# A pairwise outer-product batch norm: stores in halves, ScalarE adding the shift for eight pairs, short rows multiplied on VectorE

## The chip, the cores and the metric

One core of a Trainium2 chip runs the whole program. The metric is device time in microseconds (us). The kernel before takes 1895.81 us (median of three runs, 1895.78 to 1895.99). Engines are named as the profile names them: PE (TensorE), DVE (VectorE), ACT (ScalarE), POOL (GpSimd) and SP (SyncE, which only issues transfers here).

## The reference

There are 1024 samples with 39 fields of 16 numbers in each of two inputs, xi and xj. For each of the 741 pairs (row r, column c < r) the outer product of xj[r] and xi[c] is formed, normalised over the batch, and multiplied elementwise by a 16x16 matrix W:

```python
cross = xj[:, rows, :, None] * xi[:, cols, None, :]
mean = jnp.mean(cross, axis=(0, 2, 3), keepdims=True)
var = jnp.mean(jnp.square(cross - mean), axis=(0, 2, 3), keepdims=True)
normed = (cross - mean) * jax.lax.rsqrt(var + BN_EPS)
normed = normed * gamma[None, :, None, None] + beta[None, :, None, None]
out = normed[:, :, None, :, :] * W[None, None, :, :, :]
```

The output is 1024 x 741 x 256 numbers of four bytes, 777 MB; the inputs are about 6 MB. With a scale s and a shift t for each pair, the result is ((xj * (s * xi)) + t) * W.

## The kernel before, in words

The 1024 samples lie on 128 partitions, eight (called t) in each. A tile is one row r for two of the eight t, so each row has four tiles, and a tile holds 2r pairs of 256 numbers in each partition. Row 19 comes first, and then the rows go in couples: for r = 20, 21, ... 38 and each t0 the big tile (r, t0) is followed by the small tile (38 - r, t0). Row 38 has no small tile. Rows 34 to 37 are thus coupled with rows 4 to 1, and those rows are the last but one stage of the kernel; row 38 is the last.

The result is built in place in `y_sb`, which has two halves. One couple (76 pairs in all) fills a half and the next couple takes the other half, so a half is written again only when the stores of the couple before the last have landed.

The first 60 us compute s and t (statistics, not touched here). Then each tile goes through four steps:

- `scale_xi(n)` (L153): POOL multiplies xi by s into a tile `xs`. The pool that holds `xs` has two buffers (L74), taken in turn, so the `xs` of tile n + 2 lies where that of tile n lay.
- `products(n)` (L165): for each t and each of 16 values of i, `xs` is multiplied by one number of xj per partition. ACT does 12 (11 in rows over 31) of the 16 i (L137), POOL the other 4 (5) (L139).
- `finish(n)` (L214): for most pairs DVE does (y + t) * W in one instruction per pair (L233). For the last 13% of the pairs POOL adds t (one instruction each, L221) and then multiplies by W (one instruction for all of them, L225).
- `store(n, c0, c1)` (L173): SP issues the transfers. Rows to 24 leave in one piece, rows 25 to 31 in two, rows over 31 in three; in rows over 24 the last piece goes as one transfer for each t, the others as one for both.

The order of all instructions is the order in which the program emits them (`tc.manual_schedule()`), and each engine works through its own list. The loop (L433) does, for tile n: `scale_xi(n + 2)`, `finish(n)`, `products(n + 1)`. Seen from POOL, for a big tile B and its small tile S this reads: scale the next big tile's xi; add and weigh its share of B; products of S; scale the next small tile's xi; add and weigh its share of S, if there is one; products of the next B. An `xs` that is written again makes POOL wait until the products of two tiles before have been read out of it.

Of the kernel before, what the change touches and what calls it, by code (L numbers as in the profile page):

```python
# [8 lines left out]
AF = mybir.ActivationFunctionType  # L9
ALU = mybir.AluOpType  # L10
# [4 lines left out]
T = 2  # L15


ONE, TWO = 24, 31
FIRST_PIECES = ((0, 2, 8, 19), (0, 9, 19))


POOL_I, POOL_I_LONG = 4, 5
POOL_SHARE = 0.13

LOADS = (0, 1, 2, 4, 8)


ROW_GROUPS = (
# [5 lines left out]
def tile_pair_outer_batchnorm(  # L34
# [15 lines left out]
    nc = tc.nc  # L50
    P = nc.NUM_PARTITIONS
    NB, F, E = xi.shape
    NT = NB // P
    EE = E * E
# [7 lines left out]
    tiles = [(mid, t0, t0 // T * half // 2) for t0 in range(0, NT, T)]  # L62
# [14 lines left out]
    xj_sb = cpool.tile([P, NT, F, E], F32, name="xj_sb")  # L77
    w_sb = cpool.tile([P, 1, EE], F32, name="w_sb")
    st_sb = cpool.tile([P, 2, NP], F32, name="st_sb")
    s_sb = st_sb[:, 0:1].unsqueeze(3)  # L80
    t_sb = st_sb[:, 1]
# [39 lines left out]
    banks = [psp.tile([P, 512], F32, name=f"ps{n}") for n in range(7)]  # L121
    ps_s, ps_c, ps_g = banks[0], banks[1], banks[2:5]

    ps_st = banks[5:7] + ps_g
    stt = nc.vector.scalar_tensor_tensor

    def view(n):
        r, _, u = tiles[n]
        return y_sb[:, u : u + T * r, :].rearrange("p (t n) e -> p t n e", t=T)

    def product(n, engine, t, i, src):

        r, t0, _ = tiles[n]
        y = view(n).rearrange("p t n (i j) -> p t n i j", j=E)[:, t, :, i, :]
        scale = xj_sb[:, t0 + t, r, i : i + 1]
        if engine is nc.scalar:
            nc.scalar.activation(y, src, AF.Copy, scale=scale)  # L137
        else:
            engine.tensor_scalar(y, src, scale, 1.0, ALU.mult, ALU.mult)  # L139
# [13 lines left out]
    def scale_xi(n):  # L153
        r, t0, _ = tiles[n]
        n0 = first[r]
        xs = scaled.tile([P, T, r, E], F32, tag="xs", name=f"xs_{r}_{t0}")
        nc.gpsimd.tensor_tensor(  # L157
            xs,
            xi_sb[:, t0 : t0 + T, 0:r, :],
            s_sb[:, :, n0 : n0 + r, :].to_broadcast([P, T, r, E]),  # L160
            ALU.mult,
        )
        xs_of[n] = xs

    def products(n):  # L165

        xs = xs_of.pop(n)
        split = E - (POOL_I_LONG if tiles[n][0] > TWO else POOL_I)
        for t in range(T):
            for i in range(E):  # L170
                product(n, nc.scalar if i < split else nc.gpsimd, t, i, xs[:, t])

    def store(n, c0, c1):  # L173
        r, t0, _ = tiles[n]
        n0 = first[r]

        step = 1 if r > ONE and c1 == r else T
        for t in range(0, T, step):
            nc.sync.dma_start(  # L179
                out_v[:, t0 + t : t0 + t + step, (n0 + c0) * EE : (n0 + c1) * EE],  # L180
                view(n)[:, t : t + step, c0:c1, :].rearrange("p t n e -> p t (n e)"),
            )

    def affine(n):

        r = tiles[n][0]
        y = view(n)
        for c in range(r):
            s_c = st_sb[:, 0, first[r] + c : first[r] + c + 1]
            t_c = t_sb[:, first[r] + c : first[r] + c + 1]  # L190
            if c % 2 == 0:
                nc.scalar.activation(y[:, :, c, :], y[:, :, c, :], AF.Identity, bias=t_c, scale=s_c)  # L192
            else:
                nc.gpsimd.tensor_scalar(  # L194
                    y[:, :, c, :], y[:, :, c, :], s_c, t_c, ALU.mult, ALU.add
                )

    def weigh(n, bounds):

        y = view(n)  # L200
        for c0, c1 in zip(bounds, bounds[1:]):
            nc.vector.tensor_tensor(  # L202
                y[:, :, c0:c1, :],
                y[:, :, c0:c1, :],
                w_dve.unsqueeze(1).to_broadcast([P, T, c1 - c0, EE]),
                ALU.mult,
            )
            store(n, c0, c1)

    def bounds(r):  # L210
        pieces = 1 + (r > ONE) + (r > TWO)
        return tuple(q * r // pieces for q in range(pieces + 1))

    def finish(n):  # L214

        r = tiles[n][0]
        n0 = first[r]
        y = view(n)
        split = r - int(r * POOL_SHARE + 0.5)
        for c in range(split, r):  # L220
            nc.gpsimd.tensor_scalar(  # L221
                y[:, :, c, :], y[:, :, c, :], t_sb[:, n0 + c : n0 + c + 1], 1.0, ALU.add, ALU.mult
            )
        if split < r:
            nc.gpsimd.tensor_tensor(  # L225
                y[:, :, split:r, :],
                y[:, :, split:r, :],
                w_sb.unsqueeze(1).to_broadcast([P, T, r - split, EE]),
                ALU.mult,
            )  # L230
        for c0, c1 in zip(bounds(r), bounds(r)[1:]):
            for c in range(c0, min(c1, split)):
                stt(  # L233
                    y[:, :, c, :],
                    y[:, :, c, :],
                    t_sb[:, n0 + c : n0 + c + 1],
                    w_dve.to_broadcast([P, T, EE]),
                    ALU.add,
                    ALU.mult,
                )  # L240
            store(n, c0, c1)

    with tc.manual_schedule():
        for t0, t1 in zip(LOADS, LOADS[1:]):
            nc.sync.dma_start(xj_sb[:, t0:t1], xj_v[:, t0:t1])
# [157 lines left out]
        for r0, r1, bank, _ in ROW_GROUPS:  # L403
            n0, n1 = first[r0], first[r1 - 1] + r1 - 1
# [13 lines left out]
        def apply(group):  # L418
            ps, n0, n1 = spread_of[group]
            nc.vector.tensor_mul(ps[:, 1], ps[:, 1], st_sb[:, 0, n0:n1])  # L420
            nc.vector.tensor_mul(st_sb[:, 0, n0:n1], ps[:, 0], st_sb[:, 0, n0:n1])
            nc.vector.tensor_add(st_sb[:, 1, n0:n1], ps[:, 1], st_sb[:, 1, n0:n1])

        apply(0)
        affine(0)
        weigh(0, FIRST_PIECES[0])
        scale_xi(2)
        apply(1)
# [4 lines left out]
        for n in range(1, len(tiles)):  # L433
            if n == 1:
                products(2)
                scale_xi(3)
                continue
            if n + 2 < len(tiles):
                scale_xi(n + 2)
            finish(n)  # L440
            for group, (_, _, _, tile_of) in enumerate(ROW_GROUPS):
                if n == tile_of:
                    apply(group)
            if n + 1 < len(tiles):
                products(n + 1)
# [28 lines left out]
```

## Time and profile before

| | |
|---|---|
| median of three runs | 1895.81 us |
| profiled execution, its own time | 1895.88 us |
| its span, first to last instruction | 1894.1 us |
| DVE busy | 1730.9 us (91%) |
| ACT busy | 1621.5 us (86%) |
| POOL busy | 1574.5 us (83%) |
| PE busy | 24.5 us (1%) |
| written to memory | 776.99 MB |
| share of the 16 DMA engines' time with packets on the output queue | 97.9% |

Busy shares are means over the whole span; the limit of a stage is read from the stage. In the timeline of the profile each line is a run of like instructions of one engine: its start and length in us, the engine, the line of the kernel, what is written and read, how many, and in brackets how long the engine had been idle and what ended that. "x10" after a shape is the number of instructions. A big tile's start on DVE is the first L233 line after an idle stretch, and the distance from one to the next is the period of a couple.

### The profile page before, as it was taken

To read this page: it belongs to the slowest core of one execution; us is meant where nothing else is said; L and a number is where in the kernel's file an instruction comes from. 1 tells how busy PE (TensorE), PEld (TensorE's weight loads), DVE (VectorE), ACT (ScalarE), POOL (GpSimd) and SP (SyncE) were. 2 spreads that over 40 slices of the span, in tenths; PEclk is the share of its full clock that TensorE was granted. 3 is DMA by queue.
4 is the path that set the end of the run, shared out by engine and by line. 5 is a ranking of instruction groups with operands and counts; after the bars stand their busy time and mean duration, and the time that the engine had idled before them with its cause. 6 is when DMAs were issued, how large, how long until landed. Compare 5 with 4: busy or idle time off the path is not lost. (4 is left out here: it accounts for less than half of the span.)

```text
span 1894.1 us, 10252 instructions
## 1 busy us (share of the span) xinstructions
PE 24.5 (1%) x128; PEld 23.1 (1%) x128; DVE 1730.9 (91%) x2609; ACT 1621.5 (86%) x3625; POOL 1574.5 (83%) x1985
## 2 busy tenths in 40 slices
PE   3100000000000000000000000000000000000000
PEld 3100000000000000000000000000000000000000
DVE  7999999998989898989898989899999999999996
ACT  8998989898989897989898989888888888888762
POOL 9797878787878787878787878898888888888972
DMA  3899999999999999999999999999999999999999
GB/s 147 362 426 430 425 430 426 427 428 422 430 424 425 424 425 425 424 426 424 423 426 424 425 424 422 424 421 421 421 421 421 418 414 420 414 418 417 417 418 389
DMA packets 67567, 783.67 MB, mean 414 GB/s; under 512 B 4896, under 2 KB 6048, under 8 KB 13728
## 3 DMA queue, kind: packets, MB, share of 16 engines
q1 hardware_dynamic: 66912, 780.46, 97.9%
q10 hardware_dynamic: 576, 2.56, 0.3%
q14 instruction: 78, 0.64, 0.1%
q8 instruction: 1, 0.02, 0.0%
HBM read 6.00 MB, written 776.99 MB: 413 GB/s over the span
## 5 line engine op out<-in xcount | busy, mean ns | idle before, releaser
L233 DVE SCALAR_TENSOR_TENSOR y_sb<-y_sb,st_sb,w_dve 128x512 f32<-128x512 f32 x2542 | 1678.7, 742 | 134.9 <-issue 133.0
L137 ACT ACTIVATE y_sb<-xs,xj_sb 128x256 f32<-128x256 f32 (+32 forms) x3544 | 1576.5, 537 | 228.4 <-DMA out_dram<-y_sb 170.3
L139 POOL TENSOR_SCALAR y_sb<-xs,xj_sb 128x560 f32<-128x560 f32 (+35 forms) x1256 | 643.0, 534 | 39.4 <-DMA out_dram<-y_sb 31.1
L225 POOL TENSOR_TENSOR y_sb<-y_sb,w_sb 128x1024 f32<-128x1024 f32 (+4 forms) x138 | 441.9, 3202 | 11.5
L157 POOL TENSOR_TENSOR xs<-xi_sb,st_sb 128x576 f32<-128x576 f32 (+37 forms) x150 | 187.8, 1252 | 225.9 <-ACT y_sb L137 213.8
L221 POOL TENSOR_SCALAR y_sb<-y_sb,st_sb 128x512 f32<-128x512 f32 x384 | 259.4, 691 | 13.1 <-ACT y_sb L137 13.1
L202 DVE TENSOR_TENSOR y_sb<-y_sb,w_dve 128x1024 f32<-128x1024 f32 (+4 forms) x5 | 20.9, 4205 | 3.9 <-ACT y_sb L192 3.9
L137 ACT ACTIVATE y_sb<-xi_sb,xj_sb 128x304 f32<-128x304 f32 x40 | 18.7, 534 | 0.1
L409 PE MATMUL ps<-y_sb 39*128 39x38 f32 (+37 forms) x76 | 16.5, 397 | 5.5 <-DVE y_sb L397 5.5
L409 PEld LDWEIGHTS ps<-y_sb 39*128 39x128 f32 x76 | 16.3, 329 | 5.7 <-issue 5.7
L192 ACT ACTIVATE y_sb<-y_sb,st_sb 128x512 f32<-128x512 f32 x20 | 14.2, 798 | 0.0
L194 POOL TENSOR_SCALAR y_sb<-y_sb,st_sb 128x512 f32<-128x512 f32 x18 | 13.5, 766 | 0.3 <-issue 0.3
L139 POOL TENSOR_SCALAR y_sb<-xi_sb,xj_sb 128x304 f32<-128x304 f32 x24 | 11.9, 528 | 0.0
L294 DVE TENSOR_REDUCE y_sb<-y_sb 128x78 f32<-128x1248 f32 x8 | 11.1, 1443 | 0.0
L288 ACT ACTIVATE y_sb<-y_sb 128x1248 f32<-128x1248 f32 x8 | 9.9, 1244 | 1.3 <-POOL y_sb L278 1.3
L272 DVE TENSOR_REDUCE y_sb<-xj_sb 128x78 f32<-128x1248 f32 (+1 forms) x5 | 5.9, 1189 | 5.5 <-DMA xj_sb<-in_r_xj_dram 5.5
L278 POOL TENSOR_TENSOR y_sb<-xj_sb,y_sb 128x1248 f32<-128x1248 f32 x4 | 9.3, 2322 | 1.9 <-ACT y_sb L322 1.9
L278 POOL TENSOR_TENSOR y_sb<-xi_sb,y_sb 128x1248 f32<-128x1248 f32 x4 | 9.3, 2329 | 0.0
L311 PE MATMUL ps<-y_sb 128*39 128x79 f32 x48 | 7.2, 339 | 16.6 <-DVE y_sb L294 16.6
L311 PEld LDWEIGHTS ps<-y_sb 128*39 128x39 f32 x48 | 6.1, 183 | 17.5 <-DVE y_sb L294 9.6
L272 DVE TENSOR_REDUCE y_sb<-xi_sb 128x78 f32<-128x1248 f32 (+1 forms) x5 | 5.9, 1186 | 0.1
L254 POOL TENSOR_SCALAR_AFFINE_SELECT y_sb<-y_sb 39x4992 f32<-39x4992 f32 x1 | 4.6, 4624 | 0.0
(45 smaller groups left out, 16.9 us busy)
## 6 DMA issues: line engine op xcount, KB each, us to landing
out_dram<-y_sb SPq DMA_DIRECT2D x32, 3072.0 KB, 13.7
out_dram<-y_sb SPq DMA_DIRECT2D x29, 2816.0 KB, 15.5
out_dram<-y_sb SPq DMA_DIRECT2D x32, 1664.0 KB, 14.3
out_dram<-y_sb SPq DMA_DIRECT2D x16, 3328.0 KB, 17.1
out_dram<-y_sb SPq DMA_DIRECT2D x12, 3840.0 KB, 17.6
out_dram<-y_sb SPq DMA_DIRECT2D x29, 1536.0 KB, 15.4
out_dram<-y_sb SPq DMA_DIRECT2D x12, 3584.0 KB, 18.4
out_dram<-y_sb SPq DMA_DIRECT2D x20, 1792.0 KB, 17.7
```

What stands on the lines that cost most here:

```text
L137: nc.scalar.activation(y, src, AF.Copy, scale=scale)
L139: engine.tensor_scalar(y, src, scale, 1.0, ALU.mult, ALU.mult)
L157: nc.gpsimd.tensor_tensor(xs, xi_sb[:, t0 : t0 + T, 0:r, :], s_sb[:, :, n0 : n0 + r, :].to_broadcast([P, T, r, E]), ALU.mult,)
L192: nc.scalar.activation(y[:, :, c, :], y[:, :, c, :], AF.Identity, bias=t_c, scale=s_c)
L194: nc.gpsimd.tensor_scalar(y[:, :, c, :], y[:, :, c, :], s_c, t_c, ALU.mult, ALU.add)
L202: nc.vector.tensor_tensor(y[:, :, c0:c1, :], y[:, :, c0:c1, :], w_dve.unsqueeze(1).to_broadcast([P, T, c1 - c0, EE]), ALU.mult,)
L221: nc.gpsimd.tensor_scalar(y[:, :, c, :], y[:, :, c, :], t_sb[:, n0 + c : n0 + c + 1], 1.0, ALU.add, ALU.mult)
L225: nc.gpsimd.tensor_tensor(y[:, :, split:r, :], y[:, :, split:r, :], w_sb.unsqueeze(1).to_broadcast([P, T, r - split, EE]), ALU.mult,)
L233: stt(y[:, :, c, :], y[:, :, c, :], t_sb[:, n0 + c : n0 + c + 1], w_dve.to_broadcast([P, T, EE]), ALU.add, ALU.mult,)
L278: nc.gpsimd.tensor_tensor(devs[n % 7], sources[x][:, t0 : t0 + T], shift[:, x : x + 1, :].unsqueeze(3).to_broadcast([P, T, F, E]), ALU.sub ...
L311: nc.tensor.matmul(acc[0:F, 0 : 2 * F + 1], lhs, fb[:, t], start=t == 0, stop=t == NT - 1)
L409: nc.tensor.matmul(ps[:, :, first[r] - n0 : first[r] - n0 + r], pick[:, r, :], stq[:, :, 0:r], start=True, stop=True,)
```

## The change

Four things change.

- `bounds`: rows over 24 leave in two pieces; there is no third piece any more for rows over 31.
- `products`: the limit from which POOL takes five of the 16 i instead of four moves from rows over 31 to rows over 33. Rows of up to 4 are no longer multiplied by ACT and POOL: DVE forms all of a t's products in one instruction, two per tile, from `xs` and from a copy of four rows of xj that ACT makes once, in PSUM (`xj_short`).
- `finish`: in rows over 33 the pairs that don't go through DVE are eight instead of four or five, and they are the last eight of the first half of the row instead of the last of the row. ACT adds t to them (eight instructions), and POOL multiplies by W in two instructions of four pairs each. Rows to 33 keep the old way.
- DVE's part in rows over 33 falls from r - 4 (row 34) or r - 5 pairs to r - 8.

```diff
-ONE, TWO = 24, 31
+ONE, LONG = 24, 33
...
-POOL_SHARE = 0.13
+POOL_SHARE, POOL_PAIRS_LONG = 0.13, 8
...
+SHORT = 4
...
+    xj_short = ps_c.rearrange("p (t r i) -> p t r i", t=NT, i=E)
...
         xs = xs_of.pop(n)
-        split = E - (POOL_I_LONG if tiles[n][0] > TWO else POOL_I)
+        r, t0, _ = tiles[n]
+        if r <= SHORT:
+            for t in range(T):
+                nc.vector.tensor_tensor(
+                    view(n)[:, t].rearrange("p n (i j) -> p n i j", j=E),
+                    xs[:, t].unsqueeze(2).to_broadcast([P, r, E, E]),
+                    xj_short[:, t0 + t, r - 1 : r, :].unsqueeze(3).to_broadcast([P, r, E, E]),
+                    ALU.mult,
+                )
+            return
+        split = E - (POOL_I_LONG if tiles[n][0] > LONG else POOL_I)
...
-        pieces = 1 + (r > ONE) + (r > TWO)
+        pieces = 1 + (r > ONE)
...
-        split = r - int(r * POOL_SHARE + 0.5)
-        for c in range(split, r):
-            nc.gpsimd.tensor_scalar(
-                y[:, :, c, :], y[:, :, c, :], t_sb[:, n0 + c : n0 + c + 1], 1.0, ALU.add, ALU.mult
-            )
-        if split < r:
+        long = r > LONG
+        p1 = r // 2 if long else r
+        p0 = p1 - (POOL_PAIRS_LONG if long else int(r * POOL_SHARE + 0.5))
+        step = POOL_PAIRS_LONG // 2 if long else r
+        for c0 in range(p0, p1, step):
+            c1 = min(c0 + step, p1)
+            for c in range(c0, c1):
+                t_c = t_sb[:, n0 + c : n0 + c + 1]
+                if long:
+                    nc.scalar.activation(y[:, :, c, :], y[:, :, c, :], AF.Identity, bias=t_c)
+                else:
+                    nc.gpsimd.tensor_scalar(
+                        y[:, :, c, :], y[:, :, c, :], t_c, 1.0, ALU.add, ALU.mult
+                    )
             nc.gpsimd.tensor_tensor(
-                y[:, :, split:r, :],
-                y[:, :, split:r, :],
-                w_sb.unsqueeze(1).to_broadcast([P, T, r - split, EE]),
+                y[:, :, c0:c1, :],
+                y[:, :, c0:c1, :],
+                w_sb.unsqueeze(1).to_broadcast([P, T, c1 - c0, EE]),
                 ALU.mult,
             )
         for c0, c1 in zip(bounds(r), bounds(r)[1:]):
-            for c in range(c0, min(c1, split)):
+            for c in [*range(c0, min(c1, p0)), *range(max(c0, p1), c1)]:
...
         affine(0)
+        nc.scalar.copy(xj_short, xj_sb[:, :, 1 : SHORT + 1, :])
         weigh(0, FIRST_PIECES[0])
```

## The prediction

> **What bounds the kernel now.** I read first the slices of the page, which set DMA beside the engines:
>
> ```profile
> DVE  7999999998989898989898989899999999999996
> ACT  8998989898989897989898989888888888888762
> POOL 9797878787878787878787878898888888888972
> DMA  3899999999999999999999999999999999999999
> GB/s 147 362 426 430 425 430 426 427 428 422 430 424 425 424 425 425 424 426 424 423 426 424 425 424 422 424 421 421 421 421 421 418 414 420 414 418 417 417 418 389
> ```
>
> From the third slice on DMA is full, and no engine is full all the time. The output queue is the bound. Its rate sinks in steps: about 425 GB/s, 421 from 1210 us on (rows over 31, three pieces), then some 417. The same in stages, cut at a big tile's start:
>
> ```profile
> 1309.00:1401.00 92.00, 0.00 (x0) 0.00 (x0) 85.43 (x130) 76.15 (x174) 81.67 (x108) 1.00 1.01 422
> ...
> 1401.00:1786.15 385.15, 0.00 (x0) 0.00 (x0) 349.04 (x528) 320.90 (x740) 334.12 (x420) 1.00 1.00 417
> 1786.15:1894.10 107.95, 0.00 (x0) 0.00 (x0) 87.25 (x132) 46.03 (x66) 62.73 (x56) 1.00 0.97 406
> ```
>
> The columns are stage, length, then PE, PEld, DVE, ACT and POOL busy, clock, DMA share and GB/s. The middle line holds rows 34 to 37, where nearly all of the change acts: DVE is busy 349 of 385 us, POOL 334. So I next looked at who waits for whom, POOL above all, since it is in three of the four steps of a tile:
>
> ```profile
> POOL xs L157 <- ACT y_sb L137: 213.8, 75, 4.9
> ACT y_sb L137 <- DMA out_dram<-y_sb: 170.3, 56, 8.9
> DVE y_sb L233 <- issue: 133.0, 54, 6.1
> ```
>
> The first line is the reuse of `xs`: 75 times POOL stands at `scale_xi(n + 2)` until the products of tile n have been read, and all that is behind it in POOL's list stands too. Today that happens for big tiles alone, and the engine awaited is ACT. One couple of rows 35 and 3 in the timeline of POOL and DVE shows where the small tile stands:
>
> ```profile
> 1522.62 2.10 POOL L157 TENSOR_TENSOR xs<-xi_sb,st_sb 128x1120 f32<-128x1120 f32 x1 [3.41 <-ACT y_sb L137]
> 1524.70 3.36 POOL L221 TENSOR_SCALAR y_sb<-y_sb,st_sb 128x512 f32<-128x512 f32 x5
> 1528.14 5.60 POOL L225 TENSOR_TENSOR y_sb<-y_sb,w_sb 128x2560 f32<-128x2560 f32 x1
> 1533.72 2.22 POOL L139 TENSOR_SCALAR y_sb<-xs,xj_sb 128x48 f32<-128x48 f32 x8
> 1536.03 0.35 POOL L157 TENSOR_TENSOR xs<-xi_sb,st_sb 128x96 f32<-128x96 f32 x1
> 1536.36 7.09 POOL L139 TENSOR_SCALAR y_sb<-xs,xj_sb 128x560 f32<-128x560 f32 x10
> ...
> 1522.57 21.81 DVE L233 SCALAR_TENSOR_TENSOR y_sb<-y_sb,st_sb,w_dve 128x512 f32<-128x512 f32 x33 [2.41 <-issue]
> 1546.68 6.01 DVE L233 SCALAR_TENSOR_TENSOR y_sb<-y_sb,st_sb,w_dve 128x512 f32<-128x512 f32 x9 [2.31 <-issue]
> ```
>
> The big tile starts on DVE at 1522.57. POOL scales the next small tile's xi (128x96) at 1536.03 with no wait, and then does its ten products of the next big tile, done at 1543.45; the next tile starts on DVE at 1546.68. POOL is 3.2 us ahead of need.
>
> [...] the trace's 1024-element tensor_tensor with W from PSUM (L202) took 1222 ns[...].
>
> **The change part by part.** Call d the moment a big tile starts on DVE.
>
> *Products of rows to 4.* For a couple the change takes 24 products from ACT and 8 from POOL (2.22 us for row 3) and puts two instructions on DVE, after the big tile's pairs. What counts is the wait that moves. `scale_xi` of the next small tile, in the iteration of this small tile S, reuses S's `xs`, so it now waits for DVE's two products, which stand in DVE's list behind all pairs of the big tile. Behind that `scale_xi` in POOL's list are POOL's share of S (row 4 only) and the ten products of the next big tile; and DVE, which takes whole pairs, can't start the next big tile without these ten. That closes a loop: DVE pairs of B, DVE products of S, POOL scaling of the next S, POOL products of the next B, DVE again. Its length for each row:
>
> - a pair on DVE: 21.81/33 = 0.661 us, times r - 8;
> - two products of 256 x (38 - r) elements [...];
> - `scale_xi` of the small tile in the trace: 0.41, 0.35, 0.29, 0.24 us;
> - row 4 only: POOL's one pair of S, add and weigh, 2.02 us (start 1415.27 to the next instruction at 1417.29);
> - ten POOL products: 6.96 (8 took 5.57), 7.09, 7.22, 7.36 us;
> - two crossings between engines at 0.12 us, an estimate: at 1786 us ACT's end to POOL's start was 0.14, to DVE's 0.08.
>
> Row 34: 17.19 + 2.45 + 0.41 + 2.02 + 6.96 + 0.24 = 29.3. Row 35: 17.85 + 1.91 + 0.35 + 7.09 + 0.24 = 27.4. Row 36: 18.51 + 1.38 + 0.29 + 7.22 + 0.24 = 27.6. Row 37: 19.17 + 0.85 + 0.24 + 7.36 + 0.24 = 27.9. Four couples each make 448.8; the last turn scales row 38's xi (2.27 for 0.24) and does its products (7.49), and three turns change row, together 2.4: 451.2 us from the first tile of row 34 to the first of row 38. Before, these starts are at 1403.12 and 1786.15: 383.0, 23.9 a couple. So **+68.2 us**. DMA has 38 pairs of two t at 0.617 us (262,144 B at 425 GB/s), 23.5 us a couple, and falls behind the loop: it has gaps.
>
> The DVE products are the unknown. [...] At nothing, -26 us (two of 0.4 to 1.2 us in each of 16 couples). [...]
>
> *ScalarE's adds and POOL's weighing.* Eight adds of 0.71 us (20 such on L192 took 14.2) are 5.7 us on ACT, against some 5.5 us of small products that leave it; ACT begins the next big tile's products after them and needs 14.4 to 14.9 us, so it is ready by d + 21, inside the loop. POOL scales xi (2.1 us), then weighs four pairs twice (4.52 us each, the 128x2048 row), done at d + 12, where it then waits for DVE at d + 20: hidden in rows 34 to 37. Adding t and weighing there before took 9.0. Without the loop's cover POOL would be as late as before, not later.
>
> *Pieces.* In rows 32 and 33 (190 us) the rate should go from 421 to the 424.7 of rows with two pieces: **-1.6 us**. ACT's two more products there (1.3 us a tile) fit into its idle 4 us a couple. In rows 34 to 37 nothing is gained, as DMA is no longer the bound.
>
> *Row 38.* The first half needs POOL's second weighing, d + 12.1, and DMA's data begins about 1 us later; DVE ends at d + 19.8. With d0 = 0, the second tile starts after ACT's adds and products (5.7 + 15.3 + 0.1): 21.2. Tile 0 is on DMA from 13.1 to 36.5, the first t of its second half out at 30.7 and landed at about 32.3; its half of the buffer then takes products, so d2 = 47.8; tile 1 likewise frees at 55.7, d3 = 71.2. The last tile's data runs 84.3 to 107.8; before, 2.6 us lay between the last data (1891.5) and the end: 110.4 against 107.95 today, **+2.5 us**.
>
> *The copy of xj* takes 0.7 us on ACT while DMA isn't yet full (0.86 in 50 to 100 us): 0 to 0.7, taken **+0.4**.
>
> Sum: 68.2 - 1.6 + 2.5 + 0.4 = +69.5 on a span of 1894.1: 1963.6. The profiled execution has 1.8 us around its span, and its 1895.88 lies 0.1 over the median: **1965 us**.
>
> **Rivals.**
>
> *The wait on `xs` is covered and DMA stays the bound.* Then rows 34 to 37 go from 417 to 424.7 GB/s (-7.0), rows 32 and 33 give 1.6, row 38 and the copy cost 2.9: -5.7, 1890 us, faster. For it speaks the full DMA and that DVE's work per couple shrinks to about 20.5 us. It decides where POOL's ten products begin by d + 16, so that loop and transfers balance; DVE's list puts them at d + 20. Chance 0.06.
>
> *DVE's products run at half rate*: the loop with +21 us, 1986. For it: no such operand form is in the trace; against: L202. Chance 0.07.
>
> *The halves bind without the loop.* The first t of a last piece has 19 rows for 13, 1.9 us more, and the half of the buffer comes back later; DVE's 2 us less pay for most of it. At 0.5 us a couple for 20 couples, +10: 1906. Chance 0.04.
>
> That the change does not do what it says would need another order than the list's; DVE and POOL keep it in all of the timeline above. 0.01, near no change.
>
> **How the numbers follow.** The loop has 0.82, with its own range of 1952 to 1978 (0.5 us a turn, and part of the unknown product time). The range of 1950 to 1987 takes in the slow products too. A measurement tells 0.2% (3.8 us) from no change: faster 0.05, within 0.02, slower 0.93, of which the first rival supplies the faster and part of the same.
>
> **What would show it.** POOL L157 of small tiles waiting 8 us or so on DVE, 15 or 16 times; DVE idle 7 us before each big tile of rows 34 to 37, ended by POOL L139; periods of 27 to 29 us there and some 24 in row 38; DMA share near 0.86 in that stage; rows to 33 hardly changed. Wrong: if that wait isn't there, or DVE's products differ much from 0.4 to 1.2 us.

## The result, and the profile after

The changed kernel takes 1957.08 us (median of five runs, 1956.82 to 1957.32) against 1895.81 us before: a ratio of 1.0323, 95% interval 1.0309 to 1.0337. Its profiled execution spans 1955.4 us, 61.3 more than before. (In its numbering L161 is `scale_xi`, L143 a POOL product, L141 an ACT product, L175 the new DVE product, L243 the new add on ACT, L248 POOL's weighing and L256 the DVE pair.)

The slices of the page of the changed kernel:

```profile
DVE  7999989898989898988989898989967877777685
ACT  8998989898999889898989888899866766677683
POOL 9797879797879788887878787888776677666773
DMA  3899999999999999999999999999987889888899
GB/s 156 356 427 428 428 431 425 431 424 421 429 424 424 425 425 425 425 424 424 423 427 423 424 424 424 413 424 424 421 377 331 343 362 390 361 358 355 354 407 409
```

Up to the 29th slice, about 1400 us, little has changed. From there DMA is no longer full, and in rows 34 to 37 DVE, ACT and POOL all have a smaller busy share than before: all of them wait. The stages, with the columns as above (length, PE, PEld, DVE, ACT and POOL busy, clock, DMA share, GB/s), cut at the first big tile of row 34 and the first of row 38:

```profile
1401.59:1847.67 446.08, 0.00 (x0) 0.00 (x0) 339.63 (x509) 313.62 (x481) 308.15 (x232) 1.00 0.86 364
1847.67:1955.40 107.73, 0.00 (x0) 0.00 (x0) 79.36 (x120) 65.95 (x98) 62.99 (x40) 1.00 0.92 393
```

Row 34 begins at 1401.59, 1.5 us earlier than before (1403.12). Rows 34 to 37 take 446.1 us for 383.0. Row 38 takes 107.7 for 107.95. So -1.5 + 63.1 - 0.2 is the whole difference of 61.3 us (rounded). The DMA share of 0.86 in rows 34 to 37 is the one that the prediction named. What the engines waited for, longest in total first:

```profile
POOL xs L161 <- DVE y_sb L175: 129.1, 16, 8.3
ACT y_sb L243 <- POOL y_sb L143: 128.5, 16, 9.9
...
DVE y_sb L256 <- POOL y_sb L143: 105.9, 16, 9.1
```

All three have 16 occurrences, one for each couple of rows 34 to 37. POOL waits for DVE, and DVE and ACT for POOL. One turn, row 35 with row 3, in the timelines of POOL and of DVE:

```profile
1520.07 9.03 POOL L248 TENSOR_TENSOR y_sb<-y_sb,w_sb 128x2048 f32<-128x2048 f32 x2 [0.48 <-ACT y_sb L243]
1537.11 0.35 POOL L161 TENSOR_TENSOR xs<-xi_sb,st_sb 128x96 f32<-128x96 f32 x1 [8.00 <-DVE y_sb L175]
1537.44 7.09 POOL L143 TENSOR_SCALAR y_sb<-xs,xj_sb 128x560 f32<-128x560 f32 x10
...
1517.44 17.86 DVE L256 SCALAR_TENSOR_TENSOR y_sb<-y_sb,st_sb,w_dve 128x512 f32<-128x512 f32 x27 [7.45 <-POOL y_sb L143]
1535.22 1.81 DVE L175 TENSOR_TENSOR y_sb<-xs,ps 128x768 f32<-128x768 f32 x2
...
1544.56 15.89 DVE L256 SCALAR_TENSOR_TENSOR y_sb<-y_sb,st_sb,w_dve 128x512 f32<-128x512 f32 x24 [5.43 <-POOL y_sb L143]
```

POOL has weighed its eight pairs at 1529.1 and then stands 8.00 us at the scaling of the next small tile's xi, until DVE has done 27 pairs and the two short products (1537.03). Its ten products of the next big tile are done at 1544.53, and DVE starts that tile at 1544.56, 27.12 us after the one before. (The last line is cut off where the view ended; the tile has 27 pairs like the one before.) In the kernel before, POOL did the same ten products with no wait ahead of them.

### The profile page after: what moved, and what is told of

It is laid out like the page before. It is cut to its first block, busy times and chain, and to the rows that moved or that the text cites. A ratio compares the mean times of both kernels' runs of the same rounds, so it can differ in the third digit from the quotient of the medians.

```text
span 1955.4 us, 9554 instructions
## 1 busy us (share of the span) xinstructions
PE 24.5 (1%) x128; PEld 23.1 (1%) x128; DVE 1713.5 (88%) x2577; ACT 1646.7 (84%) x3418; POOL 1538.1 (79%) x1765
## 5 line engine op out<-in xcount | busy, mean ns | idle before, releaser
L256 DVE SCALAR_TENSOR_TENSOR y_sb<-y_sb,st_sb,w_dve 128x512 f32<-128x512 f32 x2478 | 1638.1, 741 | 209.8 <-POOL y_sb L143 105.9
L141 ACT ACTIVATE y_sb<-xs,xj_sb 128x320 f32<-128x320 f32 (+20 forms) x3176 | 1502.5, 566 | 139.0 <-DMA out_dram<-y_sb 117.2
L143 POOL TENSOR_SCALAR y_sb<-xs,xj_sb 128x352 f32<-128x352 f32 (+25 forms) x1112 | 597.7, 561 | 41.6 <-DMA out_dram<-y_sb 33.2
L248 POOL TENSOR_TENSOR y_sb<-y_sb,w_sb 128x2048 f32<-128x2048 f32 (+3 forms) x158 | 514.8, 3264 | 33.0 <-ACT y_sb L243 23.2
L161 POOL TENSOR_TENSOR xs<-xi_sb,st_sb 128x576 f32<-128x576 f32 (+37 forms) x150 | 187.8, 1252 | 314.0 <-ACT y_sb L141 172.2
L243 ACT ACTIVATE y_sb<-y_sb,st_sb 128x512 f32<-128x512 f32 x160 | 100.2, 708 | 128.9 <-POOL y_sb L143 128.5
L245 POOL TENSOR_SCALAR y_sb<-y_sb,st_sb 128x512 f32<-128x512 f32 x288 | 194.9, 692 | 0.0
L175 DVE TENSOR_TENSOR y_sb<-xs,ps 128x1024 f32<-128x1024 f32 (+3 forms) x32 | 24.7, 813 | 0.0
L141 ACT ACTIVATE y_sb<-xi_sb,xj_sb 128x304 f32<-128x304 f32 x40 | 18.7, 534 | 0.1
L206 ACT ACTIVATE y_sb<-y_sb,st_sb 128x512 f32<-128x512 f32 x20 | 14.3, 799 | 0.0
L208 POOL TENSOR_SCALAR y_sb<-y_sb,st_sb 128x512 f32<-128x512 f32 x18 | 13.5, 766 | 0.3 <-issue 0.3
L143 POOL TENSOR_SCALAR y_sb<-xi_sb,xj_sb 128x304 f32<-128x304 f32 x24 | 11.9, 532 | 0.0
```

Source lines behind the costliest of these rows:

```text
L161: nc.gpsimd.tensor_tensor(xs, xi_sb[:, t0 : t0 + T, 0:r, :], s_sb[:, :, n0 : n0 + r, :].to_broadcast([P, T, r, E]), ALU.mult,)
L175: nc.vector.tensor_tensor(view(n)[:, t].rearrange("p n (i j) -> p n i j", j=E), xs[:, t].unsqueeze(2).to_broadcast([P, r, E, E]), xj_short ...
L245: nc.gpsimd.tensor_scalar(y[:, :, c, :], y[:, :, c, :], t_c, 1.0, ALU.add, ALU.mult)
L248: nc.gpsimd.tensor_tensor(y[:, :, c0:c1, :], y[:, :, c0:c1, :], w_sb.unsqueeze(1).to_broadcast([P, T, c1 - c0, EE]), ALU.mult,)
L256: stt(y[:, :, c, :], y[:, :, c, :], t_sb[:, n0 + c : n0 + c + 1], w_dve.to_broadcast([P, T, EE]), ALU.add, ALU.mult,)
```

## Experiments

The theory is the loop of the prediction: DVE's pairs, DVE's short products, POOL's scaling of the next small `xs`, POOL's products, DVE again. The rivals are the halves, the adds on ACT, and the load of the engines.

**Short rows back on ACT and POOL.** The changed kernel with `SHORT = 0`, and without the copy of xj:

```diff
-SHORT = 4
+SHORT = 0
...
-        nc.scalar.copy(xj_short, xj_sb[:, :, 1 : SHORT + 1, :])
```

> The changed kernel with rows of up to 4 multiplied by ScalarE and GpSimd again; all else as changed. Theory (the loop over the scaled xi of the small tile): the wait of GpSimd on VectorE is gone, and the couples of rows 34 to 37 fall from 27 to 29 us to what ScalarE needs for one: eight adds 5.0, small products 5.4, big products 14.5, together 25.0 us; 16 couples make 400 us for 446, so about 1911 us. Rival (the halves, the adds and the later store cost the time): the time stays near 1957 us.

Measured: 1909.44 us, ratio 1.0072 (1.0058 to 1.0086). In rows 34 to 37 POOL no longer waits for DVE, and a couple of row 35 takes 24.87 us. That the new bound is ACT is seen in the stage of rows 34 to 37 (ACT is the fifth column, 397 of 399 us busy):

```profile
1401.00:1800.00 399.00, 0.00 (x0) 0.00 (x0) 314.79 (x477) 397.24 (x865) 342.20 (x361) 1.00 0.95 402
```

So 48 of the 61 us go when the short products leave DVE. The 13.6 us that remain against the kernel before have another cause: with the eight adds and the small products both in its list, ACT is the bound.

**The short products alone,** in the kernel before:

```diff
+SHORT = 4
...
+        if r <= SHORT:
+            for t in range(T):
+                nc.vector.tensor_tensor(...)
+            return
...
+        nc.scalar.copy(xj_short, xj_sb[:, :, 1 : SHORT + 1, :])
```

> The kernel before with only this added: products of rows to 4 on VectorE, with the copy of four rows of xj. Theory: the loop now has VectorE's r - 5 pairs (r - 4 in row 34) instead of r - 8, so it is even longer than in the whole change: 31.7, 29.2, 29.4 and 29.7 us a couple in rows 34 to 37, 482 us for 383, about 1995 us. Rival (short products are harmless, the rest of the change costs): 1896 us.

Measured: 1991.41 us, ratio 1.0505 (1.0490 to 1.0519). This part alone is worse than the whole change, as a loop with three more pairs in it (four in row 34) must be. A couple of row 35 takes 29.10 us (DVE starts at 1529.82 and 1558.92), 1.98 more than 27.12, and three pairs of 0.661 us are 1.98. Rows 34 to 37 take 480.3. The wait is the same one, and longer:

```profile
1551.47 0.35 POOL L161 TENSOR_TENSOR xs<-xi_sb,st_sb 128x96 f32<-128x96 f32 x1 [10.46 <-DVE y_sb L175]
```

**Another buffer for every second small `xs`.** The order and the instructions are those of the changed kernel:

```diff
-        xs = scaled.tile([P, T, r, E], F32, tag="xs", name=f"xs_{r}_{t0}")
+        tag = "xs_odd" if r <= SHORT and t0 // T % 2 else "xs"
+        bufs = 1 if tag == "xs_odd" else 2
+        xs = scaled.tile([P, T, r, E], F32, tag=tag, bufs=bufs, name=f"xs_{r}_{t0}")
```

> The changed kernel, but every second small tile of rows to 4 has its scaled xi in a buffer of its own, so that the scaling of a next small tile never waits for the products of the small tile just before. Same instructions, same order. Theory: in rows 35 to 37 the wait of GpSimd on VectorE goes and a couple takes 23.5 to 24 us; in row 34 GpSimd still has one pair of the small tile to add and weigh, which needs VectorE's products just as much, and stays at 28.6 us; 4 x 28.6 + 12 x 23.8 = 400 us for 446, about 1911 us. Rival (not the buffer but the order or VectorE's load): near 1957 us.

Measured: 1907.96 us, ratio 1.0064 (1.0049 to 1.0079). From the starts on DVE, row 34 takes 28.6 us a couple and rows 35 to 37 take 23.5. So the wait is one for a buffer, and where there is a second reason to wait for the same products, the loop stays closed. The timeline of POOL in row 34 shows both: the scaling runs at 1413.21 with no wait, and the add for the small tile's own pair, right behind it, takes the wait over:

```profile
1413.21 0.41 POOL L163 TENSOR_TENSOR xs<-xi_sb,st_sb 128x128 f32<-128x128 f32 x1
1421.17 0.69 POOL L247 TENSOR_SCALAR y_sb<-y_sb,st_sb 128x512 f32<-128x512 f32 x1 [7.55 <-DVE y_sb L177]
```

**The short products first in DVE's list.** The changed kernel, with the products of the small tile ahead of the big tile's pairs:

```diff
+            early = n + 1 < len(tiles) and tiles[n + 1][0] <= SHORT
+            if early:
+                products(n + 1)
             finish(n)
...
-            if n + 1 < len(tiles):
+            if n + 1 < len(tiles) and not early:
                 products(n + 1)
```

> The changed kernel with the products of the small tile (rows to 4) ahead of the big tile's pairs in VectorE's list, instead of behind them; nothing else moved. Theory: VectorE does them while it waits for the big tile, GpSimd finds the buffer free at d + 12, and rows 34 to 37 are bound by the transfers again at 23.5 to 23.8 us a couple: 378 us for 446, about 1890 us, faster than the kernel before by about 0.3%. Rival (the halves hold the buffer half longer and cost 0.5 us a couple): 1900 to 1906 us.

Measured: 1889.79 us, ratio 0.9969 (0.9956 to 0.9981): with one call moved, the change is faster than the kernel before, and 67 us faster than as it stood. The call emits DVE instructions only, so no other engine's list is altered; neither the halves nor the adds have changed. Rows 34 to 37 take 377.95 us (1401.48 to 1779.43), and DMA is full again there:

```profile
1401.00:1780.00 379.00, 0.00 (x0) 0.00 (x0) 336.72 (x508) 316.59 (x482) 307.96 (x233) 1.00 1.00 422
```

DVE does the short products right after the previous tile, and the ten POOL products of row 35 begin at 1531.01 instead of 1537.44 in a turn that starts at 1519.00, at d + 12 instead of d + 20:

```profile
1530.68 0.35 POOL L161 TENSOR_TENSOR xs<-xi_sb,st_sb 128x96 f32<-128x96 f32 x1
1531.01 7.10 POOL L143 TENSOR_SCALAR y_sb<-xs,xj_sb 128x560 f32<-128x560 f32 x10
```

**Fewer POOL products in the loop.** The changed kernel with

```diff
-POOL_I, POOL_I_LONG = 4, 5
+POOL_I, POOL_I_LONG = 4, 3
```

> The changed kernel with GpSimd taking three instead of five of the 16 i in rows over 33 (six products a tile instead of ten; ScalarE takes the other four). Theory (GpSimd's products are a link of the loop): each of the 16 couples of rows 34 to 37 is shorter by four products of 0.70 to 0.74 us, 2.8 us, until ScalarE's 22 us or the transfers' 23.5 would bind; 45 us less there, some 3 more in row 38, where ScalarE's products stand in the path: about 1915 us. Rival (the turn has a length that doesn't depend on GpSimd's products): 1957 us.

Measured: 1915.09 us, ratio 1.0103 (1.0089 to 1.0117). The turn of row 35 is 24.30 us (DVE starts 1507.64, 1531.94), 2.82 less than 27.12, for four products of 0.71. POOL still waits 8.0 us for DVE there, and six products follow:

```profile
1527.32 0.35 POOL L161 TENSOR_TENSOR xs<-xi_sb,st_sb 128x96 f32<-128x96 f32 x1 [8.01 <-DVE y_sb L175]
1527.65 4.26 POOL L143 TENSOR_SCALAR y_sb<-xs,xj_sb 128x560 f32<-128x560 f32 x6
```

Shortening one link shortens the loop by just that much and leaves the wait where it was.

**Halves alone,** in the kernel before:

```diff
-        pieces = 1 + (r > ONE) + (r > TWO)
+        pieces = 1 + (r > ONE)
```

> The kernel before with rows over 31 leaving in halves instead of thirds, and nothing else. If the third piece itself lowers the transfer rate (425 to 421 and then 417 GB/s), rows 32 to 37 give back 5 us: 1890 us. If the rate depends on the gaps and not on the pieces, the later and larger last piece costs about what the fewer pieces save: 1894 to 1898 us.

Measured: 1890.92 us, ratio 0.9975 (0.9966 to 0.9985). The pages' lines on the output queue say what was saved; first the kernel before, then this one (packets; then packets, MB and share of the 16 engines' span):

```profile
DMA packets 67567, 783.67 MB, mean 414 GB/s; under 512 B 4896, under 2 KB 6048, under 8 KB 13728
...
q1 hardware_dynamic: 66912, 780.46, 97.9%
```

```profile
DMA packets 59950, 783.66 MB, mean 415 GB/s; under 512 B 4448, under 2 KB 5600, under 8 KB 13280
...
q1 hardware_dynamic: 59296, 780.46, 97.8%
```

The same bytes in 7616 fewer packets: 448 of them under 512 B, which is 16 for each of the 28 transfers saved (one in each tile of rows 32 to 38), and 7168 of data, which is 28 times 128 partitions times two t. 97.9% of 1894.1 us is 1854.3, 97.8% of 1889.5 is 1847.9: 6.4 us less of packet time, which is 13 ns for each packet saved on each of 16 engines (6.4 x 16 / 7616). The shares are rounded, so the 6.4 is good to some 2 us, and the packet to 9 to 18 ns. From 1401 to 1780 us, nearly all of rows 34 to 37, the rate rises from 417 to 420 GB/s, not to 425.

**Thirds again in the kernel with the short products first:**

```diff
-        pieces = 1 + (r > ONE)
+        pieces = 1 + (r > ONE) + (r > TWO)
```

> The kernel with the short products ahead in VectorE's list, with thirds again in rows over 31. If the halves are what makes that kernel faster than the kernel before, it goes back by 4 to 5 us, to 1894 us; if it is the work taken from VectorE, it stays at 1890 us.

Measured: 1895.36 us, ratio 0.9999 (0.9991 to 1.0007). Without the halves nothing that can be told from noise is left of the gain. Reckoned as above, packet time is 97.9% of 1893.6 us here and 97.9% of 1888.1 with halves: 5.4 us, 11 ns for a packet.

**No adds on ACT in the kernel with the short products first:**

```diff
-        long = r > LONG
+        long = False
```

> The kernel with the short products ahead in VectorE's list, but rows over 33 finished the old way: GpSimd adds and weighs the last four or five pairs, VectorE has three more pairs a tile. VectorE then has 33 pairs and the short products in a couple, 21.8 + 0.8 to 2.3 = 22.6 to 24.1 us, about what the transfers take (23.6), with a hand-over before each tile: 24 to 24.5 us a couple, 1896 to 1902 us. If VectorE's load doesn't matter, 1890 us.

Measured: 1890.58 us, ratio 0.9974 (0.9964 to 0.9984); the expectation of 1896 to 1902 missed. The stage of rows 34 to 37 (DVE is the fourth column):

```profile
1401.00:1780.00 379.00, 0.00 (x0) 0.00 (x0) 370.70 (x561) 235.87 (x353) 300.13 (x293) 1.00 1.00 422
```

DVE is busy 370.7 of 379 us and DMA's share is still 1.00. I had charged a hand-over before each big tile on top of DVE's work. In row 35 there is none, as POOL's and ACT's products are ready ahead: a turn takes 23.46 us (DVE starts at 1520.42 and 1543.88), which is DVE's 33 pairs and two products with no gap, and just about what the transfers take (38 pairs of 262,144 B at 422 GB/s, 23.6 us). So the pairs taken from DVE by the adds buy 0.8 us, less than can be told from nothing. Nor do the short products on DVE gain anything in their better place: the halves alone took 1890.92 us.

## Why the prediction was right

The likeliest case was 1965 us in a range of 1950 to 1987; measured are 1957.1. The mechanism was the one foreseen, and the 8 us between the two are not the rest of larger errors that cancel: the loop and row 38 both came out shorter than worked out. Point by point, in the order of its sum:

- *The loop*, +68.2 us predicted, +63.1 measured (446.1 against 451.2 us for the 16 turns). Its place, its direction and its 16 waits are as said (POOL 8 us on DVE, DVE idle 5.4 to 9.1 us before each of those tiles), and its links were tested one by one: the buffer (another one opens the loop), the order on DVE (the moved call opens it), DVE's pairs (three more make it 2 us longer), POOL's products (four fewer make it 2.8 us shorter). Predicted per turn were 29.3, 27.4, 27.6 and 27.9 us for rows 34 to 37; measured are 28.94, 27.12, 27.33 and 27.53, taken from successive starts on DVE.
- The terms that were too large in a turn of row 35: the two crossings between engines were put at 0.24 us and took 0.11 (1537.03 to 1537.11, and 1544.53 to 1544.56); the two DVE products were priced at 1.91 and took 1.81, and the first began 0.08 before the pair ahead of it had ended. That is 0.31 us a turn, 16 times 5 us. Two products are the second number in each sum of the prediction: 2.45, 1.91, 1.38 and 0.85 us for rows 4 to 1. The five lengths of L202 in the kernel before, products with W in PSUM, lead to the same numbers within 0.01 us (1222 ns is the 1024 elements, 6022 the 5632):

```profile
L202 DVE TENSOR_TENSOR y_sb<-y_sb,w_dve x5: 1222/4945/6022, 40.0 to 58.5; 128x1024 f32<-128x1024 f32 x1, 128x3072 f32<-128x3072 f32 x1, 128x5632 f32<-128x5632 f32 x1, 128x4608 f32<-128x4608 f32 x1
```

A straight line through these two has 1.04 ns for an element and gives, as an estimate, 1222, 955, 689 and 422 ns for one product of rows 4 to 1. That it would hold for the broadcast operands too was my estimate; no trace of the kernel before shows it. It did: the mean of one (L175) is 1212, 947, 679 and 413 ns. But two in a row overlap a little and take 2.34, 1.81, 1.28 and 0.75 us. The fear of half the rate (the rival of 1986 us, 1.04 ns more for each of 20480 elements) was unfounded: a product of row 3 would then have taken some 1.75 us, and it took 0.947.

- *Before row 34*: predicted -1.6 + 0.4, measured -1.5. The copy is as said: in the run with the short products alone row 34 starts 0.34 later than before (1403.46). The reason given for the -1.6 isn't borne out: from 1205 to 1401 us the rate was to rise to 424.7 GB/s, and it is 421 after and 422 before. That this term came out near is luck as far as these runs show, and what lets row 34 start earlier stays open.
- *Row 38*: predicted +2.5, measured -0.2. The eight adds were priced at 0.71 us each and take 5.01 us together (0.63 each, where the mean of one is 0.708), since neighbours overlap; and DMA gave the half of the buffer back sooner than worked out: ACT could go on at d + 30.7 instead of 32.3, and the third and fourth tile start at d + 46.1 and d + 70.1 instead of 47.8 and 71.2. The other 1.6 us lie behind the fourth start: the last tile's data runs from about 12.3 to 35.6 us after it instead of 13.1 to 36.6, and 2.0 us follow instead of 2.6.
- *Halves without the loop* were given as a possible loss of 10 us by the later last piece. They are a gain: 4.7 us alone, and 5.6 in the kernel with the short products first (1895.36 to 1889.79).
- The rival of 1890 us, in which the wait on `xs` is covered, describes the kernel with the moved call, and the point given for it, POOL's ten products by d + 16, held: they begin at d + 12 there. That its time fits to a microsecond is partly luck: rows 34 to 37 gave 5.1 us instead of 7.0 (422 GB/s, not 424.7), and row 38 cost 0.7 us (108.7 for 107.95) instead of 2.5.

The kernel after is thus three parts of which one is a gain (halves, 5 us), one is neutral once nothing else stands in the way (adds), and one closes a loop because of where its instructions stand, and is neutral too when they stand elsewhere. What remains open is whether the 11 to 13 ns per packet are a property of the packet or of what comes with each transfer, since pieces, transfers and packets were changed together; no run separates them.

## What to carry to other kernels

When work moves from one engine to another, look up who reuses its input buffer. The reader's place in the new engine's list sets when that buffer comes free, and all that stands behind the waiting refill on the refilling engine moves with it (here POOL's ten products, which began at d + 20, and at d + 12 with the call moved). Moved to the end of the list of an engine that waits for that same refilling engine, a 2 us job made a loop of 27 us; at the head of the list, in a gap that was there anyway, it cost nothing. And work out the turn link by link from the timeline (start to start, not the mean length of one instruction): here each turn of rows 34 to 37 came out within 2%.

## What I had not expected

- Instructions in a row on ACT and on DVE cost less here than their mean length: eight adds of 708 ns each by the profile's page take 5.01 us, 0.63 us each; two DVE products of 768 elements, 947 ns each, take 1.81 us.
- Leaving in two pieces of 16 to 19 KB instead of three of 10 to 13 KB per partition is worth 5 us of 1895 (0.25%), some 11 to 13 ns per packet.
- DVE ran a stage of 379 us at 98% with the transfers also full (422 GB/s); two bounds at the same pace cost nothing extra here (1890.58 us, against 1890.92 with DVE at 92%).
